# Fewer stores in a graph net, its inputs asked two tiles ahead, and 92 instead of 88 graphs on the routed path

## Chip, cores and metric

The kernel runs on one core of a Trainium2 chip. The time is the device time of one execution in microseconds (us). A core has five engines with instruction streams of their own: TensorE (PE in the profile; PEld is its weight load), VectorE (DVE), ScalarE (ACT), GpSimd (POOL) and SyncE (SP). Each runs its instructions in order. SP issues nearly all plain DMA transfers here, POOL the indirect ones (gathers and scatters by a list of rows) and those that add to what lies at the target.

## What is computed

One layer on 128 graphs of 128 nodes with 256 features, so 16,384 nodes, all in float32. First a graph net, then a feed-forward layer of four experts whose gate is a graph attention over 1,048,576 random edges between all nodes.

```python
# graph net, on xn = layernorm(x)
aggregated = einsum('bnm,bmd->bnd', adj, xn)
h = relu(((1 + eps) * xn + aggregated) @ W1 + b1)      # 256 -> 512
x1 = x + h @ W2 + b2                                   # 512 -> 256
# feed-forward, on xn2 = layernorm(x1)
h = (xn2 @ W_gat).reshape(M, 4, 4)                     # 4 heads, 4 experts
e = leaky_relu(a_src[src] + a_dst[dst], 0.2)           # per edge and head, self loops too
alpha = softmax of e over the edges of one dst
agg = segment_sum(h[src] * alpha, dst)                 # 16 numbers per node
scores = layernorm(agg).reshape(.., 4, 4).mean(heads)
topk_s, topk_i = top_k(scores, 2); w = softmax(topk_s)
for ei in range(4):
    g = where(topk_i == ei, w, 0).sum(-1)
    out += g * (gelu(xn2 @ W1[ei] + b1[ei]) @ W2[ei] + b2[ei])
result = x1 + out
```

Each node needs only two of the four experts, but which two is known only after the attention over the edges.

## The kernel before

**Stage 1, graph net (L2002 to 2190).** The nodes are worked in `NT` = 32 tiles of `G` = 4 graphs. This stage is scheduled automatically: the program is written tile by tile, and every engine runs its share in the order written. A tile goes through five functions.

- `load(t)`: x into `xt` (L2022, SP; three buffers), the scaled identity into `at` (L2031, SP; two buffers), and the adjacency added on top of it by an accumulating transfer (L2032, POOL).
- `gather_rows`: layernorm (L1962 to 1973, DVE and ACT), the bias added into `xt` by an accumulating transfer (L2086, POOL), the product with the adjacency (L2090, PE), the copy to `h_t` (L2095, ACT).
- `hidden`: W1 (L2103, PE) and relu (L2107, ACT).
- `outputs`: W2 (L2114, PE), the residual add (L2119, DVE), and the stores of x1 to `x1_d` (L2120) and, for the first `NL // G` = 22 tiles, to columns 256 to 511 of the table of routed rows `xr` (L2122).
- `turned` and `rows`: the second layernorm, the store of its result to columns 0 to 255 of `xr` for the first 22 tiles (L2128), the transposes (L2133, PE) and copies (L2136, ACT), the store of the transposed rows to `xn_d` (L2137), and the 24 numbers per node that the attention needs (L2144, PE), stored to `table` (L2151).

The loop (L2155 on) interleaves the tiles: `hidden(t)`, then `load(t + 1)` and `gather_rows` of it, then `turned(t - 2)`, `outputs(t)`, `rows(t - 2)`. So the load of a tile is issued directly ahead of its own layernorm. At tile 12 the experts' weights are loaded (`load_late`), at tile 24 two zero columns are stored for each tile of `xr`. Beside all this DVE sorts the million edges by destination (`sort_edges`, L212 to 500; its last instruction stands at L499). The profile's names differ a little from the program's: x1 appears as `x` and its store as `x_d<-x`.

**Stage 2, experts, attention and routing.** The order on PE, DVE, ACT and POOL is written out statically. A planner, `Plan`, runs generators (tasks) against assumed costs and emits each engine's instructions in the order that it finds; the instructions then wait for each other by semaphores. Six tasks matter.

- *Dense tile-experts* (`Experts`). The nodes of tiles `NL // G` to 31, 10 tiles before, go through all four experts before the gate is known: 40 tile-experts, each with a first layer (L1613, gelu at L1617), a second layer (L1632), the bias (L1626) and a store of y (L1653). The tile's input comes from `xn_d`.
- *Attention.* 13 blocks of `CB` = 46 edge columns: POOL gathers the sources' rows (`hs`, L889), DVE and ACT compute the messages (L1060 to 1165; the last one is L1146), and a running sum per destination is stored to `states`. A histogram of the edges (`count`, L700 to 783) goes ahead of it.
- *Ends and pieces.* For each range of graphs in `PIECES`, once the attention has passed the blocks that `PARTS` names, the sums at the ends of each destination's segment are fetched (L1232 to 1275) and turned into gates (L1291 to 1370). `Routes.note` writes down which pair of experts each node chose.
- *Lists* (`Routes.task`, L1432 to 1582). `REACH` says up to which graph each list reaches: 32, 52, 72 and 88. The nodes are grouped by their pair of experts (six pairs) into units of 256 nodes. A pass goes over all graphs from 0 up to its reach, with one mask per graph (L1540, `low`, DVE) and three per batch of five graphs (L1547 to 1555, `high`, DVE), small matmuls (L1525), and at the end the node numbers (L1571) and places (L1578). Nodes that fill no whole unit are left to the next list. The four lists have 11, 10, 10 and 16 units (`LISTED`), 47 in all.
- *Routed units.* For each unit POOL gathers 256 rows of `xr` (L889, `r_x`), SP loads the weights of its two experts (L1733, L1739), PE transposes (L1762; copy to `m_xn` at L1766, ACT), runs the first layer (L1781; gelu L1787) and the second (L1632), DVE weighs and adds (L1804, L1814), and POOL scatters the rows to the output (L896).
- *Sums* (`stored`). Once the gates of a dense tile are known, SP reloads the four y (L2352) and x1 (L2350), DVE adds them up (L2364) and SP stores the rows (L2371).

After that a flag says whether the lists had room for every node; only if not, `general_path` computes everything again. With these inputs it isn't entered.

Of the kernel before, what the change touches and what calls it, by code (L numbers as in the profile page):

```python
# [13 lines left out]
F32 = mybir.dt.float32  # L14
# [11 lines left out]
P = 128  # L26
D = 256
# [7 lines left out]
NT = 32  # L35
G = 4
# [52 lines left out]

PARTS = [  # L90
    (14, 0, 2), (24, 0, 3), (32, 0, 4), (42, 0, 5), (52, 2, 6), (64, 3, 7),
    (72, 3, 8), (84, 4, 9), (88, 4, 10), (106, 5, 11), (116, 7, 12), (128, 7, 13),
]
PARTS = [
    (slice(start, stop), slice(a * CB, b * CB))
    for start, (stop, a, b) in zip([0] + [g for g, _, _ in PARTS], PARTS)
]
PIECES = [slice(a, b) for a, b in zip(
    (0, 32, 52, 72, 88, 106), (32, 52, 72, 88, 106, 128)
)]  # L100
MOST = 32
EARLY = 4


REACH = (32, 52, 72, 88)
NL = REACH[-1]
PAIRS = [(a, b) for a in range(X) for b in range(a + 1, X)]
SLOTS = 2 * P
# [1730 lines left out]
def adj_ffn_kernel(  # L1839
# [22 lines left out]
    nc = tc.nc  # L1862
# [145 lines left out]
    with tc.tile_pool(name="gw", bufs=1) as gw, tc.tile_pool(  # L2008
# [11 lines left out]
        def load(t):  # L2020
            xt = gp.tile([P, G, D], F32, name="xt", bufs=3)
            nc.sync.dma_start(xt, x_tiles[t])  # L2022
            at = gp.tile([P, G, P], F32, name="at")
            if t == 0:
                nc.sync.dma_start(at, adj_tiles[t])
                nc.vector.tensor_tensor(
                    at, at, self_eye[:, None, :].to_broadcast([P, G, P]), op=ALU.add
                )
                return xt, at

            nc.sync.dma_start(at, self_eye[:, None, :].to_broadcast([P, G, P]))  # L2031
            nc.gpsimd.dma_start(at, adj_tiles[t], accum_op=ALU.add)  # L2032
            return xt, at
# [49 lines left out]
        def gather_rows(xt, at):  # L2083

            xn = layer_norm(gp, xt, "xn")
            nc.gpsimd.dma_start(xt, b2_sb[:, None, :].to_broadcast([P, G, D]), accum_op=ALU.add)  # L2086
            p_h = ps_big.tile([P, 2, G * P], F32, name="big")
            for k in range(2):
                for s in range(G):
                    nc.tensor.matmul(  # L2090
                        p_h[:, k, s * P : (s + 1) * P], xn[:, s, k * P : (k + 1) * P],
                        at[:, s, :], start=True, stop=True,
                    )
            h_t = gp.tile([P, 2, G * P], F32, name="h_t", bufs=1)
            nc.scalar.copy(h_t, p_h)  # L2095
            return xt, h_t
# [13 lines left out]
        def outputs(t, xt, hid):  # L2110
            p_y = ps_big.tile([P, G, D], F32, name="big")
            for s in range(G):
                for f in range(DH // P):
                    nc.tensor.matmul(  # L2114
                        p_y[:, s, :], hid[:, f, s * P : (s + 1) * P], w2_sb[:, f, :],
                        start=(f == 0), stop=(f == DH // P - 1),
                    )
            x1 = gp.tile([P, G, D], F32, name="x1", bufs=3)
            nc.vector.tensor_tensor(x1, xt, p_y, op=ALU.add)  # L2119
            nc.sync.dma_start(x1_tiles[t], x1)  # L2120
            if t < NL // G:
                nc.sync.dma_start(xr_tiles[t][:, :, D : 2 * D], x1)  # L2122
            return x1

        def turned(t, x1):
            xn = layer_norm(gp, x1, "xn2")
            if t < NL // G:
                nc.sync.dma_start(xr_tiles[t][:, :, 0:D], xn)  # L2128
            xn_t = gp.tile([P, 2, G * P], F32, name="xn_t", bufs=1)
            for k in range(2):  # L2130
                pt = ps_hid.tile([P, G * P], F32, name="p_hid")
                for s in range(G):
                    nc.tensor.transpose(  # L2133
                        pt[:, s * P : (s + 1) * P], xn[:, s, k * P : (k + 1) * P], ident
                    )
                nc.scalar.copy(xn_t[:, k], pt)  # L2136
            nc.sync.dma_start(xn_d[t], xn_t.rearrange("p k n -> p (k n)"))  # L2137
            return xn_t

        def rows(t, xn_t):  # L2140
# [10 lines left out]
            nc.sync.dma_start(table_tiles[t], row)  # L2151


        sums = gather_rows(*loaded)
        made = []  # L2155
        for t in range(NT):
            xt, h_t = sums
            hid = hidden(h_t)
            if t == 0:
                load_row_weights()  # L2160
            if t + 1 < NT:
                sums = gather_rows(*load(t + 1))
            if t > 1:
                xn_t = turned(t - 2, made.pop(0))
            x1 = outputs(t, xt, hid)
            made.append(x1)
            if t > 1:
                rows(t - 2, xn_t)
            if t == 12:
                load_late(x1[:, 0, 0:1])  # L2170
            if t == 24:

                zeros = const.tile([P, G, 2], F32, name="zeros")
                nc.vector.tensor_single_scalar(
                    zeros, x1[:, :, 0:2], 0.0, op=ALU.mult
                )
                for to in xr_tiles:
                    nc.sync.dma_start(to[:, :, 2 * D :], zeros)
                pad = const.tile([WIN, ROW], F32, name="no_rows")
                nc.gpsimd.memset(pad, 0.0)  # L2180
                for to in states:
                    nc.sync.dma_start(to[NB * (to.shape[0] // NB) :], pad)
# [204 lines left out]
    with tc.If(flag > 0):  # L2387
        general_path(
            tc, nc, c, edges, table, dram, ident, gate, (w1, b1, w2, b2), xn_d, x1_tiles,
            out_tiles,  # L2390
        )


# [11 lines left out]


def general_path(
    tc, nc, c, edges, table, dram, ident, gate, weights, xn_d, x1_tiles, out_tiles
):

    with tc.tile_pool(name="g_fin", bufs=1) as fp:
        fin = fp.tile([P, NB, ROW], F32, name="gfin")
        general_attention(tc, nc, edges, table, dram, ident, fin)
        with tc.tile_pool(name="g_rt", bufs=1) as rt:
            steps(gates(nc, c, rt, fin, gate, NB))
    w = Consts()
    with tc.tile_pool(name="g_mw", bufs=1) as mw, tc.tile_pool(
        name="g_moe", bufs=2
    ) as mp, tc.tile_pool(name="g_big", bufs=2, space=PSUM) as ps_big, tc.tile_pool(
        name="g_hid", bufs=3, space=PSUM  # L2420
    ) as ps_hid:
        expert_tiles(w, mw)
        load_experts(nc, w, *weights[0:3])
        w.b2 = mw.tile([P, X, D], F32, name="g_b2")
        nc.sync.dma_start(w.b2, weights[3][None].to_broadcast([P, X, D]))
        with tc.For_i(0, NT, 1) as t:
            xn = mp.tile([P, 2, G * P], F32, name="g_xn")
            nc.sync.dma_start(
                xn, xn_d[ds(t, 1)].rearrange("o p (k n) -> (o p) k n", k=2)
            )  # L2430
            acc = mp.tile([P, G, D], F32, name="g_acc")
            nc.sync.dma_start(acc, x1_tiles[ds(t, 1)].rearrange("o p s d -> (o p) s d"))
            g = mp.tile([P, G, X], F32, name="g_gate")
            nc.vector.tensor_copy(g, gate[:, ds(t * G, G), :])
            for e in range(X):
                hid = mp.tile([P, DH // P, G * P], F32, name="g_hid")
                for f in range(DH // P):
                    p_hid = ps_hid.tile([P, G * P], F32, name="g_phid")
                    for k in range(2):
                        nc.tensor.matmul(  # L2440
                            p_hid, w.w1[:, e, k, f * P : (f + 1) * P], xn[:, k, :],
                            start=(k == 0), stop=(k == 1),
                        )
                    nc.scalar.activation(
                        hid[:, f, :], p_hid, AF.Gelu, bias=w.b1[:, e, f : f + 1]
                    )
                p_y = ps_big.tile([P, G, D], F32, name="g_y")
                for s in range(G):
                    for f in range(DH // P):
                        nc.tensor.matmul(  # L2450
                            p_y[:, s, :], hid[:, f, s * P : (s + 1) * P], w.w2[:, e, f, :],
                            start=(f == 0), stop=(f == DH // P - 1),
                        )
                y = mp.tile([P, G, D], F32, name="g_out")
                nc.vector.tensor_tensor(
                    y, p_y, w.b2[:, e, None, :].to_broadcast([P, G, D]), op=ALU.add
                )
                for s in range(G):
                    nc.vector.scalar_tensor_tensor(
                        acc[:, s, :], y[:, s, :], g[:, s, e : e + 1], acc[:, s, :],  # L2460
                        op0=ALU.mult, op1=ALU.add,
                    )
            nc.sync.dma_start(out_tiles[ds(t, 1)].rearrange("o p s d -> (o p) s d"), acc)


def general_attention(tc, nc, edges, table, dram, ident, fin):
# [313 lines left out]
```

## Time and profile before

Three runs took 2264.77, 2279.19 and 2255.61 us, median 2264.77. The profile is of one more execution.

| | |
|---|---|
| profiled execution | 2285.79 us |
| its span, first to last instruction | 2284.0 us |
| granted TensorE clock, mean | 0.925 of full |
| PE busy | 1992.1 us (87%) |
| DVE busy | 1562.6 us (68%) |
| POOL busy | 1060.4 us (46%) |
| ACT busy | 846.4 us (37%) |
| moved by DMA | 320.81 MB, mean 140 GB/s |
| SP's queue (q1) | 33.8% of the time of 16 DMA engines |
| POOL's queue (q0) | 18.0% |

By stages of the same execution:

| us from the start | what runs | PE | DVE | ACT | POOL | clock | GB/s |
|---|---|---|---|---|---|---|---|
| 0 to 655 | graph net, sort | 607.1 | 555.2 | 370.7 | 87.8 | 0.97 | 191 |
| 655 to 1000 | dense experts, histogram | 324.6 | 324.4 | 96.3 | 281.3 | 0.96 | 72 |
| 1000 to 1400 | dense experts, attention, list 1 | 328.4 | 174.9 | 103.2 | 233.6 | 0.88 | 83 |
| 1400 to 1984 | routed units, attention, lists 2 to 4 | 448.9 | 302.6 | 161.6 | 338.5 | 0.87 | 121 |
| 1984 to 2285 | last units, last sums | 283.1 | 205.6 | 114.6 | 119.3 | 0.96 | 224 |

A busy share is a mean over stages whose limits differ, so what an edit is worth has to be read in its own stage: which wait ends last there. Lines of the profile name engine, line, operation and tiles, out before in; `x` with a number is a count. An idle time is put down to what released it, in the form `<-ENGINE`.

### The profile page before, as it was taken

The page shows a single profiled execution, that of the slowest core. Times are in us where ns is not written, and L with a number is a line of the kernel's source. Part 1 is how long each engine was busy: PE and PEld are TensorE (multiplying, and loading weights), DVE is VectorE, ACT ScalarE, POOL GpSimd, SP SyncE. Part 2 cuts the span into 40 slices and gives each one's busy share as a digit, 9 for nine tenths or more (in the row PEclk, how much of TensorE's full clock was granted, in tenths as well). Part 3 has the DMA queues.
Part 4 walks back from the last instruction along what each step waited for, and adds up shares of the span by engine and source line. Part 5 has one row for each costly group of instructions (what it writes and reads, how often), then busy time and mean ns, then how long its engine had stood idle before and what let it go on. Part 6 is the DMA issues. An engine that isn't in the chain of part 4 may idle for free. (4 is left out here: it accounts for less than half of the span.)

```text
span 2284.0 us, 28458 instructions
## 1 busy us (share of the span) xinstructions
PE 1992.1 (87%) x8860; PEld 1476.7 (65%) x8860; DVE 1562.6 (68%) x4173; ACT 846.4 (37%) x1567; POOL 1060.4 (46%) x1004
## 2 busy tenths in 40 slices
PE   7998989999989998996788897685879878799997
PEld 5776767767756664663555555564767666588886
DVE  4888999968999998984443333554456455567884
ACT  4877544544432222332122323222423223154332
POOL 2111111111038887884456566545656665534451
PEclk9999999999989998997899898887889889899999
DMA  8988887898421222221222544343364434457892
GB/s 196 240 227 205 203 229 195 212 193 133 107 77 52 54 55 87 94 90 24 75 46 46 168 143 123 82 126 105 108 183 144 109 107 114 116 159 245 303 342 102
DMA packets 299125, 320.81 MB, mean 140 GB/s; under 512 B 111041, under 2 KB 237267, under 8 KB 298838
## 3 DMA queue, kind: packets, MB, share of 16 engines
q1 hardware_dynamic: 231878, 241.03, 33.8%
q0 software_dynamic: 67088, 77.86, 18.0%
q8 instruction: 75, 1.23, 0.2%
q14 instruction: 84, 0.69, 0.1%
HBM read 165.03 MB, written 129.65 MB: 129 GB/s over the span
## 5 line engine op out<-in xcount | busy, mean ns | idle before, releaser
L889 POOL DMA_INDIRECT hs<-table,index x552 | 635.7, 1152 | 168.9 <-issue 166.5
L1632 PE MATMUL big<-mw,m_hid 128*128 (+1 forms) x2784 | 658.9, 392 | 31.9 <-issue 31.4
L1632 PEld LDWEIGHTS big<-mw,m_hid 128*128 128x128 f32 x2784 | 537.6, 196 | 129.9 <-issue 58.4
L1781 PE MATMUL m_phid<-m_xn,mw 128*128 128x256 f32 x1504 | 368.1, 402 | 75.5 <-ACT m_xn L1766 39.0
L1781 PEld LDWEIGHTS m_phid<-m_xn,mw 128*128 128x128 f32 x1504 | 301.4, 202 | 129.3 <-ACT m_xn L1766 40.5
L1613 PE MATMUL m_phid<-m_xn,mw 128*128 128x512 f32 x640 | 302.2, 623 | 34.7 <-ACT m_hid L1617 22.3
L1639 ACT COPY m_out<-big 128x1024 f32<-128x1024 f32 x87 | 88.1, 1013 | 583.6 <-PE big L1632 349.3
L2103 PE MATMUL p_hid<-h_t,w_sb 128*128 128x512 f32 x512 | 236.4, 613 | 18.0 <-ACT hid L2107 16.9
L1613 PEld LDWEIGHTS m_phid<-m_xn,mw 128*128 128x128 f32 x640 | 124.9, 198 | 178.3 <-issue 145.2
L1787 ACT ACTIVATE m_hid<-m_phid,r_b 128x256 f32<-128x256 f32 x376 | 154.7, 472 | 226.5 <-PE m_phid L1781 80.0
L2032 POOL DMA_DIRECT2D at<-in_adj_dram x31 | 40.6, 1309 | 420.0 <-DMA at<-self_eye 413.4
L2114 PE MATMUL big<-w_sb,hid 128*128 128x256 f32 x1024 | 228.3, 380 | 0.0
L2114 PEld LDWEIGHTS big<-w_sb,hid 128*128 128x128 f32 x1024 | 192.3, 191 | 24.7
L880 POOL COPY seen<-marks 128x1 f32<-128x1 f32 x87 | 29.5, 339 | 351.2 <-ACT marks L885 351.0
L2103 PEld LDWEIGHTS p_hid<-h_t,w_sb 128*128 128x128 f32 x512 | 96.2, 194 | 131.7 <-issue 104.4
L1617 ACT ACTIVATE m_hid<-m_phid,mb 128x512 f32<-128x512 f32 x160 | 108.2, 687 | 169.6 <-PE m_phid L1613 112.2
L1814 DVE SCALAR_TENSOR_TENSOR r_x<-m_out,r_x 128x256 f32<-128x256 f32 x188 | 86.8, 482 | 81.5 <-ACT m_out L1639 71.8
L896 POOL DMA_INDIRECT out_dram<-r_x,places x94 | 108.4, 1153 | 34.8 <-issue 21.1
L889 POOL DMA_INDIRECT r_x<-xr,nodes x94 | 100.5, 1069 | 40.5 <-issue 26.9
L2107 ACT ACTIVATE hid<-p_hid,b_sb 128x512 f32<-128x512 f32 x128 | 86.0, 679 | 55.7 <-PE p_hid L2103 55.5
L1540 DVE TENSOR_SCALAR low<-wide,part 128x128 bf16<-128x128 bf16 x244 | 44.9, 265 | 71.7 <-remote 40.0
L2090 PEld LDWEIGHTS big<-at,xn 128*128 128x128 f32 x512 | 68.1, 205 | 38.3 <-ACT xn L1973 22.5
(404 smaller groups left out, 2602.2 us busy)
## 6 DMA issues: line engine op xcount, KB each, us to landing
mw<-in_L_ffn_W_dram SPq DMA_DIRECT2D x102, 512.0 KB
states<-room SPq DMA_DIRECT2D x55, 552.0 KB
ys<-m_out SPq DMA_DIRECT2D x40, 512.0 KB
y_in<-ys SPq DMA_DIRECT2D x40, 512.0 KB
xt<-in_x_dram SPq DMA_DIRECT2D x32, 512.0 KB
xt<-b_sb POOLq DMA_DIRECT2D x32, 512.0 KB
x_d<-x SPq DMA_DIRECT2D x32, 512.0 KB
xn_d<-xn_t SPq DMA_DIRECT2D x32, 512.0 KB
```

Of the source, the lines that this page charges most:

```text
L889: self.nc.gpsimd.indirect_dma_start(out=out, out_offset=None, in_=rows, in_offset=bass.IndirectOffsetOnAxis(ap=index, axis=0),)
L896: sc = self.nc.gpsimd.indirect_dma_start(out=rows, out_offset=bass.IndirectOffsetOnAxis(ap=index, axis=0), in_=values, in_offset=None, bou ...
L1613: nc.tensor.matmul(p_hid, w1[:, k, f * P : (f + 1) * P], xn[:, k, :], start=(k == 0), stop=(k == 1),)
L1617: nc.scalar.activation(hid[:, f, :], p_hid, AF.Gelu, bias=b1[:, f : f + 1])
L1632: nc.tensor.matmul(p_y[:, s, :], hid[:, f, s * P : (s + 1) * P], w2[s // 2][:, f, :], start=(f == 0 and not b2), stop=(f == DH // P - 1 an ...
L1639: nc.scalar.copy(y, p_y)
L1781: nc.tensor.matmul(p_hid[:, half], w1[i][:, k, f * P : (f + 1) * P], xt[:, k, :], start=(k == 0), stop=(k == 1),)
L1787: nc.scalar.activation(hid[:, f, half], p_hid[:, half], AF.Gelu, bias=b1[i][:, f : f + 1])
L1814: self.nc.vector.scalar_tensor_tensor(x[:, s, D : 2 * D], y[:, 2 * i + s, :], x[:, s, 2 * D + i : 2 * D + i + 1], x[:, s, D : 2 * D], op0= ...
L2103: nc.tensor.matmul(p_hid, w1_sb[:, k, f * P : (f + 1) * P], h_t[:, k, :], start=(k == 0), stop=(k == 1),)
L2107: nc.scalar.activation(hid[:, f, :], p_hid, AF.Relu, bias=b1_sb[:, f : f + 1])
L2114: nc.tensor.matmul(p_y[:, s, :], hid[:, f, s * P : (s + 1) * P], w2_sb[:, f, :], start=(f == 0), stop=(f == DH // P - 1),)
```

## The change

Three edits.

1. *Stores of the graph net.* x1 goes to `x1_d` or to `xr`, no longer to both, and the transposed rows go to `xn_d` only for tiles that stay dense. `general_path`, which read both for all tiles, now takes the first tiles from `xr` and transposes them itself.
2. *Loads of the graph net.* `load(t + 2)` is issued after `gather_rows` of tile t + 1, where `load(t + 1)` was issued directly ahead of it. The number of buffers stays as it was, three for `xt` and two for `at`.
3. *Routing.* `REACH` becomes 32, 52, 72, 84, 92. The tiles below 92 // 4 = 23 are routed, nine stay dense: 36 tile-experts. The five lists have 11, 10, 10, 6 and 12 units, 49 in all. `PIECES` is cut at 84 and 92 instead of 88, which makes seven pieces of six, and the part of the edge sort that ended at graph 88 now ends at 92, with 5 instead of 4 as the block at which it may begin.

```diff
@@ PARTS, PIECES, REACH
-    (72, 3, 8), (84, 4, 9), (88, 4, 10), (106, 5, 11), (116, 7, 12), (128, 7, 13),
+    (72, 3, 8), (84, 4, 9), (92, 5, 10), (106, 5, 11), (116, 7, 12), (128, 7, 13),
...
-    (0, 32, 52, 72, 88, 106), (32, 52, 72, 88, 106, 128)
+    (0, 32, 52, 72, 84, 92, 106), (32, 52, 72, 84, 92, 106, 128)
...
-REACH = (32, 52, 72, 88)
+REACH = (32, 52, 72, 84, 92)
@@ outputs
-            nc.sync.dma_start(x1_tiles[t], x1)
-            if t < NL // G:
-                nc.sync.dma_start(xr_tiles[t][:, :, D : 2 * D], x1)
+            nc.sync.dma_start(
+                xr_tiles[t][:, :, D : 2 * D] if t < NL // G else x1_tiles[t], x1
+            )
@@ turned
-            nc.sync.dma_start(xn_d[t], xn_t.rearrange("p k n -> p (k n)"))
+            if t >= NL // G:
+                nc.sync.dma_start(xn_d[t], xn_t.rearrange("p k n -> p (k n)"))
@@ the loop
+        ahead = load(1)
         sums = gather_rows(*loaded)
...
             if t + 1 < NT:
-                sums = gather_rows(*load(t + 1))
+                sums = gather_rows(*ahead)
+            if t + 2 < NT:
+                ahead = load(t + 2)
@@ general_path (not entered with these inputs)
+        with tc.For_i(0, NL // G, 1) as t:
+            row = mp.tile([P, G, 2 * D], F32, name="g_row")
+            nc.sync.dma_start(
+                row, xr_tiles[ds(t, 1)][:, :, :, 0 : 2 * D].rearrange("o p s d -> (o p) s d")
+            )
...
+            layers(t, xn, acc)
```

More of the change, by code (lines that the diff above doesn't have):

```diff
@@ L2389, in adj_ffn_kernel @@
             tc, nc, c, edges, table, dram, ident, gate, (w1, b1, w2, b2), xn_d, x1_tiles,
-            out_tiles,
+            xr_tiles, out_tiles,
         )
@@ L2407, in general_path @@
 def general_path(
-    tc, nc, c, edges, table, dram, ident, gate, weights, xn_d, x1_tiles, out_tiles
+    tc, nc, c, edges, table, dram, ident, gate, weights, xn_d, x1_tiles, xr_tiles,
+    out_tiles
 ):
@@ L2425, in general_path, with layers @@
         nc.sync.dma_start(w.b2, weights[3][None].to_broadcast([P, X, D]))
[L2426 to L2432, printed above, removed]
+        def layers(t, xn, acc):
             g = mp.tile([P, G, X], F32, name="g_gate")
@@ L2463, in general_path @@
             nc.sync.dma_start(out_tiles[ds(t, 1)].rearrange("o p s d -> (o p) s d"), acc)
+        with tc.For_i(0, NL // G, 1) as t:
[3 more added lines that the diff above has]
+            )
+            xn = mp.tile([P, 2, G * P], F32, name="g_xn")
+            for k in range(2):
+                pt = ps_hid.tile([P, G * P], F32, name="g_phid")
+                for s in range(G):
+                    nc.tensor.transpose(
+                        pt[:, s * P : (s + 1) * P], row[:, s, k * P : (k + 1) * P], ident
+                    )
+                nc.scalar.copy(xn[:, k], pt)
+            acc = mp.tile([P, G, D], F32, name="g_acc")
+            nc.vector.tensor_copy(acc, row[:, :, D : 2 * D])
+            layers(t, xn, acc)
+        with tc.For_i(NL // G, NT, 1) as t:
+            xn = mp.tile([P, 2, G * P], F32, name="g_xn")
+            nc.sync.dma_start(
+                xn, xn_d[ds(t, 1)].rearrange("o p (k n) -> (o p) k n", k=2)
+            )
+            acc = mp.tile([P, G, D], F32, name="g_acc")
+            nc.sync.dma_start(acc, x1_tiles[ds(t, 1)].rearrange("o p s d -> (o p) s d"))
+            layers(t, xn, acc)
 def general_attention(tc, nc, edges, table, dram, ident, fin):
```

## Prediction

> **What bounds the kernel now.** I read the page first, then the waits of each engine before 655 us, the timeline around the hand-over to the experts, the chain of waits, and a table by stage.
>
> ```profile
> span 2284.0 us, 28458 instructions
> PE 1992.1 (87%) x8860; PEld 1476.7 (65%) x8860; DVE 1562.6 (68%) x4173; ACT 846.4 (37%) x1567; POOL 1060.4 (46%) x1004
> ```
>
> TensorE (PE) is the busiest engine, but 87% is a mean over stages with different limits. The first is the graph net with the edge sort on VectorE (DVE) beside it. Its end:
>
> ```profile
> 661.04 1.19 PE L1613 MATMUL m_phid<-m_xn,mw 128*128 128x512 f32 x1 [6.99 <-DVE over L499]
> ```
>
> The experts start when the sort's last instruction (L499) is done, 7 us after PE has run out of graph net. So both engines have to finish sooner before anything is gained. What DVE waits for in this stage, and how one such wait arises (tile 11; SP's queue, then DVE):
>
> ```profile
> DVE st L1962 <- DMA xt<-in_x_dram: 47.7, 21, 6.3
> ```
>
> ```profile
> 199.28 0.36 SPq L2128 DMA_DIRECT2D xr<-xn  x1
> 199.74 1.34 SPq L2022 DMA_DIRECT2D xt<-in_x_dram  x1
> ...
> 208.95 0.43 DVE L1962 BATCH_NORM_STATS2 st<-xt 128x6 f32<-128x256 f32 x1 [3.34 <-DMA xt<-in_x_dram]
> ```
>
> The load of x stands on SP's in-order queue behind the store of xn, which waits for ScalarE (ACT). It goes out when the tile is already due, lands 9.2 us later, and DVE, with the sort queued behind it, stands still: 47.7 us in 21 waits.
>
> In the second stage PE runs dense tile-experts (L1613, L1632), one every 14.50 us, and later routed units (L1762, L1781, L1632), one every 14.25 us:
>
> ```profile
> 1191.61 0.60 PE L1626 MATMUL big<-mb,ones 3*128 3x512 bf16 x2
> ...
> 1199.15 7.03 PE L1613 MATMUL m_phid<-m_xn,mw 128*128 128x512 f32 x16
> 1206.11 0.60 PE L1626 MATMUL big<-mb,ones 3*128 3x512 bf16 x2
> ```
>
> ```profile
> 2001.39 6.91 PE m_phid L1781 x32
> 2008.29 0.44 PE big L1762 x4
> 2008.73 6.91 PE big L1632 x32
> 2015.64 6.91 PE m_phid L1781 x32
> ```
>
> PE holds that pace only from about 1984 on. Before, DVE, ACT and GpSimd (POOL) interleave attention, gates and list building with it in one fixed order, and all wait for each other:
>
> ```profile
> 1440.00:1524.00 84.00, 54.30 (x273) 46.22 (x272) 48.72 (x193) 18.02 (x37) 38.95 (x42) 0.82 0.28 72
> 1524.00:1640.00 116.00, 90.85 (x408) 78.75 (x407) 56.55 (x161) 38.51 (x75) 69.28 (x70) 0.88 0.44 133
> 1640.00:1730.00 90.00, 66.36 (x338) 54.76 (x338) 51.76 (x197) 21.50 (x46) 50.61 (x52) 0.85 0.48 138
> 1730.00:1848.00 118.00, 102.97 (x425) 84.28 (x425) 53.90 (x158) 36.59 (x75) 76.45 (x80) 0.88 0.46 132
> 1848.00:1964.00 116.00, 93.07 (x461) 76.12 (x460) 75.37 (x264) 32.78 (x68) 65.61 (x68) 0.90 0.43 110
> ```
>
> Columns: busy us and instructions of PE, PEld, DVE, ACT, POOL, then granted clock, DMA share, GB/s. Rows one, three and five are the list passes for 52, 72 and 88 graphs. Lines 1632 and 1781 alone run 209, 384, 246, 401 and 349 matmuls in these rows; at 0.216 us each (6.91/32) that is 45, 83, 53, 87 and 75 us of work. PE therefore loses 39, 33, 37, 31 and 41 us: 46%, 41% and 35% of a pass, 28% of the time between passes.
>
> **Part 1, graph net.** *Removed:* for 23 of 32 tiles the stores of x1 (L2120) and of the transposed xn (L2137), 512 KB each: 23.6 MB of the 124.9 MB that the DMA queues move by 655 us at a mean 191 GB/s. SP saves about 0.73 us of issue in each such tile (0.378 + 0.351). The routed rows kept in xr already hold both. *Moved:* x (L2022), the scaled identity (L2031, both SP) and the accumulated adjacency (L2032, POOL) go out one tile earlier, on SP past the stores of one tile. The x load now waits for the buffer that the add of tile t-1 (L2119) frees, one tile before it is needed. On POOL the accumulate of tile t+2 follows the bias accumulate (L2086) of t+1; behind it waits only L2086 of t+2, due a tile later. POOL is 13% busy here, which covers this.
>
> PE's tiles start 18.22 us apart when nothing is late (344.63 to 362.85). From tile 2 (42.09) to tile 31 (613.25) the 29 intervals take 571.2 us against 528.4: 42.8 us too many. DVE has 47.7 us of x waits, and 555 of 655 us are work. The gain cannot exceed the smaller, 43. It could be only about 10, if DVE meets the next late thing (it also waits 12.3 us for ACT, 11.3 for PE and 9.3 for the sort's own round trip through memory). The excess intervals stand where x was late, and with x a tile early 9.2 us of latency is inside 18 us of cover. So I take 28, two thirds of the ceiling. If that cover is gone, the 47.7 comes back.
>
> **Part 2, routing.** *PE:* tile 22 becomes routed: 4 dense tile-experts less (4 x 14.50 = 58.0), 49 units for 47 (2 x 14.25 = 28.5): -29.5 us. *DVE:* one more list pass. 84 + 92 for 88 graphs means 88 more L1540 (16.1 us in the 88 pass), about 12 for the batch masks (0.25 to 0.32 us each, three per five graphs) and 13 for the fixed scans and digits: 41 us. A seventh piece of gates is some 70 instructions of 0.2 us, 14. Two units add 7.7 (16 x 0.48), four dense ones save 6.7. DVE is 52% busy from 1400 to 1984, so this fits. *POOL:* 8 indirect transfers more at 1.26 us of pitch, 10 us. *SP:* four weight loads more, four stores and reloads of y less, one store of states less. *ACT:* two more Exp calls with table loads out and back, 4 x 1.28 = 5.1 us, which PE sees through m_hid. xr gets one more zero store; the general path is not entered, so its larger code costs nothing here (instruction fetch is 0.3% of the DMA engines' time).
>
> What the added pass costs PE is not in the trace as such. Lower end: what passes lose over the 28% of the time around them, 15, 12 and 8 us, mean 12, as the attention they run in has the same 13 blocks. Upper end: all that a pass loses, 39. The nearest row is the 88 pass (excess 8, whole 41); some stretching of the stage is likely, so I take 15, nearer the lower end. With 5.5 for gates and table loads: -29.5 + 15 + 5.5 = -9 us, ends -35 (the stage's stretch shrinks with the work) and +20.
>
> The clock column speaks against the pass too: 0.82, 0.85 and 0.90 in the passes, 0.98 from 1984 on. The Trainium skill, "TensorE: Matmul & The Clock Gate", section "What's actually happening", says that an idle window of about 3.4 us puts the array to half clock. By that, if each of the 17 batches of the added pass opened such a gap, it would cost an estimated 29 us (17 x 1.7), and part 2 would come to +5. The rows lose less than that, so they decide.
>
> **Are units ever missing?** In this run each list was written well before its first unit was turned:
>
> ```profile
> 1730.09 0.18 DVE L1571 TENSOR_SCALAR nodes<-node 128x20 int32<-128x20 f32 x1
> ...
> 1964.16 0.18 DVE L1571 TENSOR_SCALAR nodes<-node 128x32 int32<-128x32 f32 x1
> ```
>
> Unit 21 was turned at 1831, unit 31 at 2025: 101 and 61 us of reserve. 58 us less dense work, stretched as the stage is, uses up about 73. The last list now feeds 12 units, not 16, and six come from the 84 list before it, so the margin is thin but there.
>
> **Sum.** -28 - 9 = -37 us. The profiled execution took 2285.8 (span 2284.0), 0.9% over the median of the three runs, 2264.8. From its own time: 2248.8; the same 37 us off the median: 2228.
>
> **Rivals.**
> 1. *The late list becomes the bound (slower).* From the start of the gates of piece 72-88 (1790) to the list (1964) is 174 us. If 84 and 92 run one whole after the other, the last list is written at 1964 + 174 - 28 = 2110. Then 10 us for its rows, 12 x 14.25 = 171, and 28 from the last unit's end to the end of the span (as now): 2319 against 2284, +35, or 2300. It decides once the list is later than 2075. For it: the lists are one task in order, and PE does slow down in passes. Against: the 84 list needs one block less, so its gates can start some 45 us sooner, and gates of 84-92 run beside it. Chance 0.10.
> 2. *Part 1 gives little:* DVE loses as much elsewhere, 5 us gained: -14, 2251. For it: an in-order DVE with a sort in between. Against: 47.7 us name one cause. Chance 0.17.
> 3. *The added pass costs all that a pass loses now:* -28 + 20 = -8, 2257. For it: the 41 us of the 88 pass. Against: the 28% are there without it. Chance 0.15.
> 4. *Nothing of the pass reaches PE:* -28 - 35 = -63, 2202. For it: from 1984 on PE is at full pace with DVE 74% busy. Against: DVE's last sums end at 2241, only 43 us ahead of the end, and 41 us of lists are put before them. Chance 0.18.
>
> My forecast keeps 0.40, with its own range 2212 to 2243.
>
> **How the numbers follow.** About 1% (23 us) can be told from no change. Faster by more: nearly all of the forecast, all of 4 and a little of 2 and 3, 0.66. Within: rivals 2 and 3 and an edge of 1, 0.24. Slower: 0.10. The range runs from below 4 (both ceilings, -43 - 35, give 2187) over 3, and leaves out most of 1: 2188 to 2276.
>
> **What would show it.** Right: the wait of L1962 on x under 10 us, L1613 first at about 633, PE tiles near 18.2 us apart, 36 dense copies and 49 units, last nodes written before 2065, unit pace 14.25 after it, span about 2247. Wrong: first L1613 after 650 (part 1), PE idle before the transposes L1762 with DVE still in L1540 (rival 1), or a loss near 40 us in each of four passes (rival 3).

## The result and the profile after

The changed kernel takes 2290.34 us (median of 20 runs, 2260.23 to 2307.99), the kernel before 2279.46 us (median of 20, the three shown above among them). The ratio is 1.0048, 95% interval 1.0025 to 1.0071: half a per cent slower, where 2228 us was forecast and 2188 to 2276 was the range. The profiled execution took 2292.86 us, its span 2290.8 us, 6.8 us over the span before.

The runs below were made in five groups, each on a chip of its own, and the kernel before took about 2020 us on two of these chips and about 2250 us on three, so a ratio is always to the kernel before in the same group, and whole times of different groups are not compared. On the chips of 2250 us the stage from 1000 to 2000 us is stretched (the last section shows what goes with it).

The page of the changed kernel:

```profile
span 2290.8 us, 28740 instructions
PE 1984.7 (87%) x8888; PEld 1477.6 (65%) x8888; DVE 1608.6 (70%) x4428; ACT 838.9 (37%) x1565; POOL 1050.9 (46%) x1010
```

PE has 29.5 us less work by the count of the prediction, but only 7 us less busy time. Busy time is not work alone: the same 8860 matmuls of 88 routed graphs took 1992.1 us in the profile before and 1911.9 us in that of `gnn_only` on a chip of 2020 us. DVE has 46 us more.

**Graph net.** The waits of DVE up to 655 us, and the load of x around 350 us (start, duration, engine, line):

```profile
DVE st L1962 <- DMA xt<-in_x_dram: 52.6, 24, 6.5
```

```profile
349.54 1.21 DVE L2119 TENSOR_TENSOR x<-xt,big 128x1024 f32<-128x1024 f32 x1
350.78 0.37 SPq L2120 DMA_DIRECT2D xr<-x  x1
351.25 0.46 SPq L2022 DMA_DIRECT2D xt<-in_x_dram  x1
...
357.66 0.43 DVE L1962 BATCH_NORM_STATS2 st<-xt 128x6 f32<-128x256 f32 x1 [1.71 <-DMA xt<-in_x_dram]
```

DVE still waits 52.6 us for x, where it waited 47.7. The load goes out 0.5 us after the residual add L2119 has ended, and 6.4 us later DVE takes up the layernorm of that very x, after waiting for it. In the instruction order of DVE the layernorm of a tile stands a few instructions behind the add of the tile three before it, in both kernels. For the kernel before the prediction shows the load and the layernorm of tile 11, at 199.74 and 208.95; the add of tile 8 there:

```profile
196.09 1.20 DVE L2119 TENSOR_TENSOR x<-xt,big 128x1024 f32<-128x1024 f32 x1
```

With three buffers, that add frees the place for the load. In tiles 3 to 14 the load went out 1.9 to 4.6 us after it in the kernel before, and 0.5 to 2.1 us after it now: asking a tile earlier moved it by about 2 us. DVE does not run its share in the order written, as I had put it ahead. As written, the add of one more tile stands ahead of each layernorm; in the changed kernel DVE takes the layernorm first in 27 of the 29 tiles from tile 3 on. The end of the stage:

```profile
657.92 13.61 PE L1613 MATMUL m_phid<-m_xn,mw 128*128 128x512 f32 x25 [6.18 <-DMA m_xn<-xn_d]
...
669.97 0.29 DVE L499 SCALAR_TENSOR_TENSOR over<-shift,over 128x128 f32<-128x128 f32 x1
```

The experts start 3 us earlier than before, and 12 us ahead of the sort's end. So the first expert matmul does not wait for L499, as I had read the profile before; it waits for its input (`m_xn`), and the two had only ended together. The sort itself ends 9.5 us later.

**Routing.** The last two lists on DVE, and PE around the last one:

```profile
1947.88 0.17 DVE L1571 TENSOR_SCALAR nodes<-node 128x12 int32<-128x12 f32 x1
2079.10 0.18 DVE L1571 TENSOR_SCALAR nodes<-node 128x24 int32<-128x24 f32 x1
```

```profile
2055.59 0.64 PE L1762 MATMUL big<-ident,r_x 128*128 128x128 f32 x4
...
2073.26 0.36 PE L1525 MATMUL pt<-high,low 128*128 128x48 bf16 x5 [3.01 <-DVE high L1555]
...
2078.47 10.61 PE L1632 MATMUL big<-mw,m_hid 128*128 x48
2088.92 0.60 PE L1762 MATMUL big<-ident,r_x 128*128 128x128 f32 x4
2090.81 7.17 PE L1781 MATMUL m_phid<-m_xn,mw 128*128 128x256 f32 x32 [1.30 <-ACT m_xn L1766]
```

The 84 list is written at 1948, the 92 list 131 us later. Only six units, 85 us of PE work, lie between them. The 37th unit (u36) is turned (L1762) at 2055.6, the next one at 2088.9, 10 us after the list: 33 us for a cycle of 14.25. PE does not stand idle right ahead of that turn (it works on L1632 until 2089.1). The planner spread the last known units over the pass, so the shortage shows as small waits inside it, such as the 3.0 us at 2073.3.

**The end.** The last sums and the last unit's rows (L1814) on DVE before, then the last rows after and the chain that ended last:

```profile
2237.86 3.26 DVE L2364 SCALAR_TENSOR_TENSOR acc<-y_in,gate,acc 128x256 f32<-128x256 f32 x8 [0.30 <-issue]
...
2270.87 1.92 DVE L1814 SCALAR_TENSOR_TENSOR r_x<-m_out,r_x 128x256 f32<-128x256 f32 x4 [3.19 <-ACT m_out L1639]
```

```profile
2271.22 1.92 DVE L1814 SCALAR_TENSOR_TENSOR r_x<-m_out,r_x 128x256 f32<-128x256 f32 x4
```

```profile
2273.06 1.74 DVE acc L2368 x5
2274.80 0.24 issue
2275.04 1.37 DVE acc L2368 x4
...
2276.62 2.92 DVE acc L2368 x8
```

Before, the last sum ended at 2241, 32 us ahead of the last unit's rows. Now 28 of the 144 sums (L2368) stand behind those rows, and the span ends 17.7 us after those rows instead of 11.2. The rows themselves are done at 2273.1, before at 2272.8: the tail is the 6.5 us of the difference, and PE's 29.5 us less of work have vanished altogether.

### The profile page after: what moved, and what is told of

Read it like the earlier page. It is cut to its first block, busy times and chain, and to the rows that moved or that the text cites. A ratio compares the mean times of both kernels' runs of the same rounds, so it can differ in the third digit from the quotient of the medians.

```text
span 2290.8 us, 28740 instructions
## 1 busy us (share of the span) xinstructions
PE 1984.7 (87%) x8888; PEld 1477.6 (65%) x8888; DVE 1608.6 (70%) x4428; ACT 838.9 (37%) x1565; POOL 1050.9 (46%) x1010
## 5 line engine op out<-in xcount | busy, mean ns | idle before, releaser
L889 POOL DMA_INDIRECT hs<-table,index x552 | 626.1, 1134 | 168.1 <-issue 163.5
L1632 PE MATMUL big<-mw,m_hid 128*128 (+1 forms) x2720 | 657.8, 396 | 49.8 <-issue 48.5
L1632 PEld LDWEIGHTS big<-mw,m_hid 128*128 128x128 f32 x2720 | 529.3, 198 | 150.5 <-issue 79.3
L1781 PE MATMUL m_phid<-m_xn,mw 128*128 128x256 f32 x1568 | 394.9, 410 | 90.0 <-ACT m_xn L1766 51.4
L1781 PEld LDWEIGHTS m_phid<-m_xn,mw 128*128 128x128 f32 x1568 | 320.0, 207 | 150.6 <-ACT m_xn L1766 55.9
L1613 PE MATMUL m_phid<-m_xn,mw 128*128 128x512 f32 x576 | 268.1, 617 | 18.8 <-ACT m_hid L1617 11.3
L1787 ACT ACTIVATE m_hid<-m_phid,r_b 128x256 f32<-128x256 f32 x392 | 161.9, 471 | 286.5 <-remote 98.1
L1613 PEld LDWEIGHTS m_phid<-m_xn,mw 128*128 128x128 f32 x576 | 112.1, 197 | 144.6 <-issue 124.5
L1617 ACT ACTIVATE m_hid<-m_phid,mb 128x512 f32<-128x512 f32 x144 | 97.6, 687 | 137.1 <-PE m_phid L1613 102.3
L889 POOL DMA_INDIRECT r_x<-xr,nodes x98 | 105.8, 1080 | 63.7 <-issue 27.0
L1540 DVE TENSOR_SCALAR low<-wide,part 128x128 bf16<-128x128 bf16 x332 | 60.9, 262 | 97.4 <-PE pt L1525 52.6
L1814 DVE SCALAR_TENSOR_TENSOR r_x<-m_out,r_x 128x256 f32<-128x256 f32 x196 | 90.5, 483 | 26.8 <-ACT m_out L1639 17.2
L1804 DVE SCALAR_TENSOR_TENSOR r_x<-b_rows,r_x 128x256 f32<-128x256 f32 x196 | 90.6, 483 | 11.0 <-issue 3.7
```

Source lines behind the costliest of these rows:

```text
L889: self.nc.gpsimd.indirect_dma_start(out=out, out_offset=None, in_=rows, in_offset=bass.IndirectOffsetOnAxis(ap=index, axis=0),)
L1613: nc.tensor.matmul(p_hid, w1[:, k, f * P : (f + 1) * P], xn[:, k, :], start=(k == 0), stop=(k == 1),)
L1617: nc.scalar.activation(hid[:, f, :], p_hid, AF.Gelu, bias=b1[:, f : f + 1])
L1632: nc.tensor.matmul(p_y[:, s, :], hid[:, f, s * P : (s + 1) * P], w2[s // 2][:, f, :], start=(f == 0 and not b2), stop=(f == DH // P - 1 an ...
L1781: nc.tensor.matmul(p_hid[:, half], w1[i][:, k, f * P : (f + 1) * P], xt[:, k, :], start=(k == 0), stop=(k == 1),)
L1787: nc.scalar.activation(hid[:, f, half], p_hid[:, half], AF.Gelu, bias=b1[i][:, f : f + 1])
```

## Experiments

Theories. **A:** the early request moves nothing, because the three buffers of x are the limit. **B:** in the second stage PE's work no longer counts; the end is the last list plus the units behind it. **C** (rival): the added pass holds up PE by itself, wherever it stands.

**Group 1 (before: 2020.5 us).** The two halves, the pass alone, and five buffers.

The graph net of the change with the routing of before:

```diff
-REACH = (32, 52, 72, 84, 92)
+REACH = (32, 52, 72, 88)      # PARTS and PIECES as before
```

> The graph net of the change (fewer stores, loads asked two tiles ahead) with the routing of before: 88 graphs, four lists. Theory A (buffers): a load of x still waits for the add that frees one of three buffers, so asking earlier moves nothing. First expert matmul at 656 to 659 us (before 661.0, after 657.9), DVE still waits 45 to 55 us for x, ratio to before 0.996 to 1.003. The step of the forecast (28 us gained in the graph net) would give a first expert matmul at about 633 and a ratio of 0.988.

Ratio 0.9998 (0.9985 to 1.0011); DVE waited 45.2 us for x; first expert matmul at 652.7, 3 us ahead of what was expected. A holds so far: this half is worth nothing.

The routing of the change with the graph net of before:

> The graph net of before with the routing of the change: 92 graphs, five lists. Theory B (late last list): the last node list is written at 2065 to 2085 us and 12 units of 14.25 us come after it, so the end is list + 10 + 171 + 28 to 38, ratio 1.000 to 1.010. The step of the forecast (9 us gained by the routing) would give a ratio of 0.996 and the last list before 2065. Theory C (the added pass holds up PE directly): the same ratio as B, but the loss is spread over the passes and PE still has units left when the last list is written.

Ratio 0.9993 (0.9981 to 1.0005), last list at 1815.4. The times expected were those of a stretched middle and don't apply to this chip; the end came 206 us after the last list, as B says (209). B and C are not told apart by this run alone.

The added pass alone, in the kernel before:

```diff
-REACH = (32, 52, 72, 88)
+REACH = (32, 52, 72, 84, 88)   # and PIECES cut at 84 and 88
```

> The kernel before with one list pass more: lists at 32, 52, 72, 84 and 88, 88 graphs routed, so the same 47 units and 40 dense tile-experts; only the pass and its piece of gates are added. Theory B: the last list comes later (2040 to 2070 us) but feeds only 10 units (142 us), so it does not set the end: ratio 0.997 to 1.004. Theory C: the pass costs PE 15 to 39 us wherever it stands: ratio 1.007 to 1.017.

Ratio 1.0005 (0.9990 to 1.0019): the pass costs 1 us, give or take 3. C falls on this chip. PE's waits for the masks of the lists, in all five passes of this kernel:

```profile
PE pt L1525 <- DVE high L1555: 6.0, 5, 1.9
```

This kernel and the one ahead of it have five passes each (the last one four graphs longer with the routing of the change), and the routing of the change has 29.5 us less of PE work. The difference between them is 0.12%, 2.4 us, and within the noise. The work that PE is spared buys next to nothing.

Five buffers for x, with the graph net of the change:

```diff
-            xt = gp.tile([P, G, D], F32, name="xt", bufs=3)
+            xt = gp.tile([P, G, D], F32, name="xt", bufs=5)
...
-            hid = gp.tile([P, DH // P, G * P], F32, name="hid")
+            hid = gp.tile([P, DH // P, G * P], F32, name="hid", bufs=1)
```

> The graph net of the change with five buffers for x instead of three (room made by one buffer for the hidden rows instead of two), routing of before. Theory A: with buffers free the load really goes out a tile earlier, DVE waits under 15 us for x, the first expert matmul comes at 625 to 645 us, and the time falls by 10 to 30 us (ratio 0.987 to 0.996). Rival A2 (x is late because the DMA queues are full, or DVE meets the next late thing): waits of DVE stay above 40 us in sum or move to others, first expert matmul after 650, ratio 0.997 to 1.005.

Ratio 0.9892 (0.9873 to 0.9911), 22 us. DVE's waits in the graph net, and the first expert matmul:

```profile
DVE sd L1966 <- ACT sd L1965: 20.9, 17, 7.1
DVE x L2119 <- PE big L2114: 16.6, 2, 10.4
DVE st L1962 <- DMA xt<-in_x_dram: 11.9, 5, 4.9
```

```profile
626.00 16.61 PE L1613 MATMUL m_phid<-m_xn,mw 128*128 128x512 f32 x32 [6.11 <-DMA m_xn<-xn_d]
```

The wait for x fell from 45.2 to 11.9 us, 14 of the 33 us came back as waits for ScalarE (7.0 to 20.9) and 5 as waits for PE (11.7 to 16.6), and the experts start 27 us earlier than with three buffers. A is shown, and so is the gain that the forecast put into the graph net.

**Group 2 (before: 2248.5 us).** The change again, a later fourth list, and the buffers without the rest.

> The changed kernel once more, beside the kernels of this group. The two halves alone gave 0.9998 (graph net) and 0.9993 (routing) where the kernel before takes 2020 us. If nothing but these two acts, the whole gives their product, 0.997 to 1.002. If the ratio of 1.005 of the result is a property of the kernel and not of the stretched middle stage there, it comes out at 1.003 to 1.007 again.

Ratio 1.0091 (1.0055 to 1.0127): slower again, by more than the 1.003 to 1.007 expected and than the product of the halves. So on a stretched chip the change costs something that its halves do not cost on the other. The whole change was never run on a chip of 2020 us.

```diff
-REACH = (32, 52, 72, 84, 92)
+REACH = (32, 52, 72, 88, 92)   # PIECES cut at 88 and 92; PARTS (88, 4, 10), (92, 5, 10)
```

> The changed kernel with its fourth list at 88 in place of 84 (lists at 32, 52, 72, 88, 92 with 11, 10, 10, 8 and 10 units). The work of PE and the number of passes stay; the fourth pass is four graphs longer, and two units more are known before the last list. Theory B (PE runs out before the last list): the gap ahead of the first unit of the last list goes from 33 to about 15 us, and the time falls by 10 to 20 us, ratio to before 0.989 to 0.996. Theory C (the pass itself costs): nothing changes, ratio 0.997 to 1.003. If the last list comes later by as much as the two units give (28 us), B gains nothing either; the time of the last list tells that.

Ratio 1.0019 (0.9983 to 1.0056), 0.7% under the change in the same group, but outside the 0.989 to 0.996 that B expected. The gap ahead of the last list shrank to 12 us as B says (copies behind the turns, L1766, at 2075.8 and 2087.9), but a new one opened ahead of the fourth, written at 1957.8: 69 us from one unit to the next (1896.3 to 1965.4). In the medians it is 14 us faster (2249.4 against 2263.9), though the two profiled spans are equal (2261.4, 2262.2); the tail behind the last rows is 12.0 us, not 17.8. So B's wait can be moved to another list, and a part of its price saved; it does not go away.

The five buffers (and one for the hidden rows) in the kernel before, with no other edit:

> The kernel before with five buffers for x (and one for the hidden rows), no other edit: loads asked one tile ahead, all stores kept. If the buffers alone were short: ratio 0.986 to 0.992 as with the changed graph net (0.989). If asking earlier and the stores matter once there are buffers, the gain is half or less: 0.994 to 1.000.

Ratio 0.9920 (0.9886 to 0.9955), wait for x 11.0 us, first expert matmul at 621.6. The buffers alone bring most of it. The first expert matmul gives no sign that the rest adds anything: with the change's graph net it came at 626.0 and 624.4 (groups 1 and 5; with three buffers the kinds of chip differ there by 2 us, 652.7 and 650.4). Whether asking two tiles ahead and storing less add something once the buffers are there (0.9892 and 0.9860 in other groups) was not compared within one group.

> The changed kernel with both: the fourth list at 88, and five buffers for x. Under A and B the two gains add: 0.978 to 0.986, the fastest of all kernels here. Under A alone: 0.987 to 0.992.

Ratio 0.9927 (0.9894 to 0.9960). This expectation was a miss, since `lists88_92` by itself had gained nothing (1.0019). Its product with the 0.9920 of the buffers is 0.994, so the buffers bring their gain here too, and routing 92 graphs with them is worth as much as routing 88.

**Group 3 (before: 2023.2 us).** A known delay in the last list pass.

> The routing of the change with the graph net of before, a second time: the group in which it gave 0.9993 ran the kernel before in 2020 us, without the stops of ScalarE between 1000 and 2000 us that the first profiles show. If the stops are there again (kernel before at 2240 to 2280 us): 1.003 to 1.010, since the two lists at the end are then paced by the stretched middle and the 29.5 us that PE saves wait for them. If they are not there: 0.997 to 1.002 as before.

Ratio 1.0001 (0.9985 to 1.0016).

> The kernel before with the added list at 84 and 88 graphs, a second time, for the same reason. Theory C (the added pass is what costs): with the stops 1.005 to 1.015, as much as the routing of the change or more. Theory B (the wait for the last list costs, the pass by itself little): 0.997 to 1.005.

Ratio 1.0003 (0.9987 to 1.0019). Both repeat group 1.

```diff
         nc.vector.tensor_tensor(found, found, pair, op=ALU.mult)
+        if n == NL:
+            for _ in range(9):
+                for _ in range(3):
+                    nc.vector.tensor_tensor(found, found, pair, op=ALU.mult)
+                yield 2.2
```

> The changed kernel with 27 needless repeats of one multiplication (0.73 us each, 20 us on DVE) put into its last list pass, the output unchanged. Theory B: the last list sets the end, so the time grows by 12 to 22 us over the changed kernel (0.6 to 1.0 percent of the kernel before). If the last list has reserve: 0 to 6 us.

Ratio 1.0169 (1.0150 to 1.0187), 34 us. The last list, and PE's turns around it (L1571 and L1762 are five lines further down in this kernel):

```profile
1839.26 0.18 DVE L1576 TENSOR_SCALAR nodes<-node 128x24 int32<-128x24 f32 x1
```

```profile
1785.40 0.64 PE L1767 MATMUL big<-ident,r_x 128*128 128x128 f32 x4
1844.95 0.45 PE L1767 MATMUL big<-ident,r_x 128*128 128x128 f32 x1 [7.70 <-DMA r_x<-xr,nodes]
```

The list came 25 us later than with the same routing in this group (1814.7), and the span ended 32 us later (2052.6 against 2020.7), 6 of them as a longer tail behind the last rows (23.5 against 17.8). The time grew by more than the delay: the last list has no reserve at all. (The comparison is with the routing alone; the rest of the change was worth nothing on such a chip.)

> The kernel before with the same 27 repeats (0.70 us each, 19 us) in its last list pass, the one for 88 graphs. Its first unit was turned 61 us after the list, so the list has reserve: ratio to before 0.998 to 1.004. If a late list costs here too, or if any work put on DVE costs its own length: 1.007 to 1.010.

Ratio 0.9969 (0.9957 to 0.9982). The same 19 us cost nothing before; the kernel even became 6 us faster, which neither theory expected. The planner laid out another order around the added steps, and which part of that order helps was not looked into. It says that 0.3% can come from the order alone, which is not much less than the loss of the change itself.

**Group 4 (before: 2249.9 us).** The halves where the middle is stretched.

> The changed kernel once more. Where the kernel before takes 2240 to 2280 us it gave 1.0048 and 1.0091: 1.003 to 1.010 again there. Where the kernel before takes about 2020 us its halves gave 0.9998 and 0.9993: 0.997 to 1.002 there.

Ratio 1.0060 (1.0027 to 1.0093).

> The routing of the change alone. If the routing is what costs where the middle stage is stretched by ScalarE's stops, it gives 1.004 to 1.011 there and the graph net alone 0.997 to 1.002. Where the kernel before takes 2020 us: 0.998 to 1.002 for the third time.

Ratio 1.0040 (1.0012 to 1.0067).

> The graph net of the change alone. If the loss where the middle stage is stretched comes from the graph net (the edge sort on DVE ended 9 us later in the changed kernel's profile): 1.003 to 1.008 there, and the routing alone 0.998 to 1.003. By the theory of the late list: 0.997 to 1.002 anywhere.

Ratio 0.9982 (0.9949 to 1.0014). The loss belongs to the routing, 9 us, as far as these intervals tell. DVE waited 43.7 us for x in `gnn_only3`.

**Group 5 (before: 2252.1 us).** Pass, delay and buffers on a stretched chip.

> The added list pass alone, with 88 graphs. Where the middle stage is stretched (kernel before at about 2250 us) the routing of the change cost 0.4 percent. Theory C, the pass costs there: 1.004 to 1.017. Theory B, the last list and the sums behind it cost: 0.996 to 1.003 here too, with 60 to 75 us of reserve between the last list and its first unit's turn. Where the kernel before takes 2020 us: 1.000 to 1.001 for the third time.

Ratio 1.0017 (0.9984 to 1.0051), 4 us, give or take 8. The interval does not shut out a few us for the pass there. The first unit of the last list was turned 78 us after the list, a little more than the 60 to 75 expected.

> The changed kernel with 20 us more on DVE in its last list pass, a second time. If the last list sets the end where the middle is stretched too: the end of the span 206 to 214 us after the last list, and a ratio to before 0.6 to 1.6 percent above the changed kernel's (1.006 to 1.009 there), so 1.012 to 1.025. If it does not: 1.003 to 1.010.

Ratio 1.0220 (1.0181 to 1.0259), 1.3 to 1.6% above the change in groups 2 and 4: no reserve there either. The end came 224 us after the list, more than the 206 to 214 expected, 6 of them in the tail.

> The graph net of the change with five buffers for x, routing of before, a second time: 0.987 to 0.994 on any chip, if what it saves in the graph net is passed on by the middle stage unchanged. DVE waits under 15 us for x, the first expert matmul at 615 to 630 us.

Ratio 0.9860 (0.9818 to 0.9903), just below what was expected; first expert matmul at 624.4. This version, the graph net of the change with five buffers and 88 graphs, beats both kernels and has the lowest ratio on both kinds of chip, but it was not run beside the other two versions with five buffers.

**All profiles side by side.** Time of the last list (DVE L1571), units behind it, end of the span, and what the units need by the sum of rival 1 (14.25 us each, with 10 us to the first matmul and 28 us behind the last):

| kernels | last list | units | end | end − list | needed |
|---|---|---|---|---|---|
| before | 1964.2 | 16 | 2284.0 | 320 | 266 |
| change's graph net alone (groups 1, 4) | 1712.9, 1910.0 | 16 | 2023.7, 2224.4 | 311, 314 | 266 |
| five buffers, 88 graphs (1, 2, 5) | 1690.4, 1913.4, 1924.4 | 16 | 2003.5, 2227.9, 2239.3 | 313 to 315 | 266 |
| before with delay | 1725.7 | 16 | 2013.6 | 288 | 266 |
| 84 and 88 (1, 3, 5) | 1773.2, 1767.7, 2008.7 | 10 | 2022.7, 2017.7, 2259.3 | 250, 250, 251 | 181 |
| change (result, 2, 4) | 2079.1, 2052.9, 2046.3 | 12 | 2290.8, 2262.2, 2254.7 | 212, 209, 208 | 209 |
| change's routing alone (1, 3, 4) | 1815.4, 1814.7, 2046.2 | 12 | 2021.6, 2020.7, 2253.6 | 206, 206, 207 | 209 |
| change with delay (3, 5) | 1839.3, 2071.6 | 12 | 2052.6, 2295.7 | 213, 224 | 209 |
| lists at 88 and 92, without and with buffers (2) | 2065.4, 2017.3 | 10 | 2261.4, 2212.0 | 196, 195 | 181 |

With 88 graphs the last list has 45 to 70 us to spare (22 with the delay); with the change's routing it has none, in six profiles from five sets of runs, whether the whole takes 2020 or 2290 us. The lists at 88 and 92 lie between, with 14 to 15 us to spare. The tail behind the last rows is 17.7 us in all six profiles of the change's routing and 11.2 with 88 graphs, also with five lists (84 and 88).

## Why the prediction was wrong, point by point

**Part 1, −28 us: wrong step, and wrong size.** It measured 0.9998 and 0.9982, so 0 to 4 us. The text named the buffer ("The x load now waits for the buffer that the add of tile t-1 (L2119) frees, one tile before it is needed") and then counted 18 us of cover anyway. There was none. The text took "one tile before it is needed" from the order in which the program is written; the automatic order sets the layernorm of a tile as early as its x can be there, right behind that add, so each tile of lead that the program asks for is spent at once. The ceiling of 43 us was of the right order for the prize: with two buffers more the kernel gained 18 to 32 us (0.8%, 1.1%, 1.4%). Rival 2, which had part 1 at 5 us, was right about it, for another reason. The reading that experts wait for the sort's L499 failed as well, see above.

**Part 2, PE's −29.5 us: right sum, no effect.** The dense part did get shorter: the first unit was turned at 1302 instead of 1375. But in the same stretch from 1440 to 2090 us, counted as in the prediction (matmuls of L1632 and L1781 at 0.216 us, turns at 0.11), PE lost 219 us where it had lost 186. The 33 us more are spread over the whole stage, in many small waits of one fixed order, not in one place. That PE is the busiest engine was true, and did not make it the limit here.

**The pass, +15 us: too much.** 1 us, give or take 3, on the chips of 2020 us; 4, give or take 8, on a stretched one. The end taken as the lower one, 12, was already above it. Rival 3, with 39 us, falls on both; rival 4 was right on the price as far as the intervals tell, and wrong that 63 us would follow.

Where this case's PE did stand long, its clock fell:

```profile
1968.03 10.09 PE L1781 MATMUL m_phid<-m_xn,mw 128*128 128x256 f32 x32 [7.97 <-ACT m_xn L1766]
```

After 8.0 us of idling 32 matmuls took 10.1 us, with a granted clock of 0.50 in the first 3.5 us; after 1.3 us (at 2090.81 above) they took 7.2, at 1.00. This agrees with the Trainium skill, "TensorE: Matmul & The Clock Gate", section "What's actually happening" (an idle window of about 3.4 us puts the array to half clock). But in the 84 pass of the changed kernel PE waited for masks once, for 0.6 us, and in all five passes of `list84` for 1.9 us at most: the 17 gaps that the estimate of 29 us supposed never opened.

**"Are units ever missing?": the step that decided.** The text took the reserve of the old last list (61 us), took 73 us of shorter dense work from it, and called what was left "thin but there", on the ground that fewer units hang on the last list. It never set the time of the new last list against the 85 us that six units last. The lists came 131 us apart (109 to 129 in the other profiles of this routing). The reserve of 101 us named beside it was read from the copy behind a turn; PE turned unit 21 at 1822.9, 93 us after its list.

**Rival 1: right mechanism, price too high.** Its rule, list + 10 + units × 14.25 + 28, gives 2288 for a list at 2079; the span ended at 2290.8. It put the list at 2110 with a gain of 28 us in the graph net already taken off, and so 2319 and a chance of 0.10. The break-even it named, 2075, held: the list came 4 us after it, and the span ended 6.8 us later than before. On the chips of 2020 us the routing alone comes out even (ratio 1.000), on a stretched one 9 us slower. What it lacked is the tail: sums that are left to DVE behind the last rows, 6.5 us. PE idle ahead of L1762, the sign named for it, did not show in that form in the profile of the changed kernel.

Of the signs named, the units and dense copies, and the unit pace after the last list came as said; the wait for x, the first expert matmul, the last list and the span did not.

## What to carry to other kernels

Before costing an earlier load, ask which instruction frees its buffer and where the consumer stands in the engine's order; if one follows the other directly, only another buffer moves the load. Where work is released in lots, compare the spacing of the lots with the work in each: a lot of 85 us cannot cover 131 us, and sparing the fed engine work makes that worse. A delay of known size put in front of the suspected limit, in both kernels, shows in two runs which of them has reserve, as long as the answer (34 us here) is well above what a new order alone can do (6 us here).

## What the runs showed of the hardware

The same program, the kernel before, took 2020 us on two chips and 2250 to 2280 us otherwise. Where it is slow, ScalarE stands still with no releaser that the profile knows ("remote"); the waits of the changed kernel from 655 us on:

```profile
ACT m_out L1639 <- remote: 113.6, 9, 20.2
ACT m_hid L1787 <- remote: 98.1, 14, 12.8
ACT m_xn L1766 <- remote: 62.2, 8, 11.9
```

All such waits of ScalarE come to 324 us before and 329 us after, 34 and 40 stops, to 255 to 354 us in the ten profiles of groups 2, 4 and 5, and to none in the eight profiles of groups 1 and 3. Their cause stays open. Why the change costs nothing in its halves on one kind of chip and half a per cent on the other is not shown. The stops may shift which of two chains is later. But with 92 graphs there are also somewhat more of them (33 to 45, against 30 to 34 with 88), and no run separates the two.
